# A graph network on one core: part of the row gathers replaced by one-hot matrix products

## The chip, the cores and the metric

The kernel runs on one core of a Trainium2 chip. The core has TensorE (matrix products, PE in the profile; its weight loads are PEld), VectorE (DVE), ScalarE (ACT), GpSimd (POOL) and SyncE (SP), and 16 DMA engines that move data between HBM and on-chip memory: SBUF, and PSUM, which has 8 banks of 512 f32 values in each of 128 partitions. Each engine works through its own instructions in order, and waits on semaphores for the others. The metric is the device time of one execution in microseconds (us), as a median of several.

## The reference

There are 12,500 nodes with 32 features and 400,000 edges `src -> dst`. Three graph attention layers follow one another on the same edges, with a residual and a layernorm; then an edge network with a maximum over the edges of each node, and again a residual and a layernorm.

```python
def _gat(x, edge_index, W, att_s, att_d, bias, heads, ch, neg_slope):
    h = (x @ W.T).reshape(n, heads, ch)
    a_s = (h * att_s[None]).sum(-1)
    a_d = (h * att_d[None]).sum(-1)
    logits = leaky_relu(a_s[src] + a_d[dst], neg_slope)
    m = segment_max(logits, dst)
    ex = exp(logits - m[dst])
    denom = segment_sum(ex, dst)
    alpha = ex / (denom[dst] + 1e-16)
    out = segment_sum(alpha[:, :, None] * h[src], dst)
    return out.reshape(n, heads * ch) + bias
...
x = layernorm(x + three layers of _gat, with elu and clip between them)
e_feat = concatenate([x[rol], x[col], edge_attr])       # rol = src, col = dst
v = relu(e_feat @ W1 + b1) @ W2 + b2
x = layernorm(x + maximum(segment_max(v, col), x))
```

What matters here are the reads by `src`: `h[src]` and `a_s[src]` in each attention layer and `x[rol]` in the edge network, one row of a node table for each of 400,000 edges, four times.

## The kernel before, in words

Edges are sorted by `dst`. Partition p of 128 holds 3125 consecutive edges, so a column t is one edge for each partition. Four stages run over the columns in chunks of T = 60 (50 chunks of 60, then 48, 32, 29 and 16): stages 1 to 3 are `attention(1)`, `(2)` and `(3)` (lines 629 to 784), stage 4 is `edge_network` (lines 805 to 901). For sorted edges the branch without `eid` runs. Sums and maxima over the edges of a node are scans along the columns.

For each column of a chunk, `gather` (line 67, recorded as line 68) issues an indirect DMA from GpSimd's queue: it brings 128 rows of the node table, one for each partition, at the indices `idx[:, t]`. Rows have 36, 34, 33 and 32 f32 values in the four stages. In stages 1 to 3 they land in `g`, of which there are four buffers (line 104); in stage 4 in `xs`, also four (line 832). There is one gather instruction a column, 3125 a stage. In stages 2 to 4 the table is written by the stage before: a table row stands at an edge's place, and `src_last` and `src_first` are the places of a source node's last and first edge; `last_i` and `first_i` hold these places by node. Table rows of chunks and of a last merge go out when they are computed, so a stage's table is complete only at the end of the stage before.

A chunk of attention, in the order of the program: gathers into `g`; the next chunk's `ad` is loaded from SP's queue; `lg` (line 697), scans for the running maximum `mx` (704), `rr` (708 to 711); then `wt`, the exponentials of `lg`, written by ScalarE into `small_p[:, :heads*n]` (715); for each head `rx` (720), the product of `g` with `wt` into `gf` (723) and ScalarE's copy of `wt` into `gf` (725); the scans on `gf` (734); `rows` copied by ScalarE and stored. In stages 1 and 2 `finish` (503) follows: `divided` (487) uses `den = small_p[:, 128:]` and adds the bias (501), which stands in PSUM in the tile `fixed`; three ScalarE passes; then for each block of 16 columns `pe`, `yb`, `yt`, two products on TensorE (`ph` 528, `pa` 529) and transposes by VectorE (531, 532). In stage 3 `finish3` (550) follows: `divided` with the bias from SBUF, the residual, and `layernorm` (537 to 548), whose row sums stand in `small_p` too.

A chunk of stage 4: gathers into `xs`; `keep` in `small_p` (849); `xf` and its scans (854, 864); for each block of 16 columns three transposes (`xt`, `et`, `xst`, 870 to 872), six products into `ph0` and `ph1` (877), two into `pv` (883), and a transpose (884); scans on `vf` (887); then `result` (798), which adds the bias from `fixed`, and `layernorm`, with row sums in `small_p`.

PSUM is full: a tile of up to 512 f32 values takes a bank. `small_p` has a bank of its own, `fixed` another.

At a stage's end `handed_on` (582) carries sums across partitions. Its tile `pt` has two halves in one bank: TensorE transposes `tops` into the second (591), VectorE scans that one (595), and TensorE transposes `nums` into the first (600). Stages 1 and 2 also scatter rows of `x0` into `x_e` there (`move`, 624).

The program is ordered by a list scheduler that gives each engine its instruction order and adds the waits that the order of the program asks for; later instructions fill an engine's gaps where nothing binds them.

Of the kernel before, what the change touches and what calls it, by code (L numbers as in the profile page):

```python
# [9 lines left out]
F32 = mybir.dt.float32  # L10
BF16 = mybir.dt.bfloat16
# [13 lines left out]
def gnn_resnorm_kernel(ctx: ExitStack, tc: tile.TileContext, a: dict, out: bass.AP):  # L25

# [56 lines left out]

    groups = [(c0, min(28, NC - c0)) for c0 in range(0, NC, 28)]
# [19 lines left out]
    gpool = gstack.enter_context(tc.tile_pool(name="g", bufs=4, side="right"))  # L104
# [4 lines left out]
    x0 = runs.tile([P, NC, D], F32, name="x0")  # L109
# [22 lines left out]
    fixed = ctx.enter_context(tc.tile_pool(name="fixed", bufs=1, space=PSUM)).tile([P, 512], F32, name="fixed")  # L132
    own = const.tile([P, 1], F32, name="own")
    nc.gpsimd.iota(own, pattern=[[1, 1]], base=E + NN, channel_multiplier=1,
                   allow_small_or_imprecise_dtypes=True)
    zeros = const.tile([P, 1250], F32, name="zeros")
# [59 lines left out]

    table1 = dram.tile([NN, D + 4], F32, name="table1")
# [10 lines left out]
    def clear(table, part=0, parts=1):  # L208
        flat = edge_rows(table).rearrange("p t w -> p (t w)")
        k = TE * table.shape[1] // parts  # L210
        z = next(z for z in range(1250, 0, -1) if k % z == 0)
        tc.keep_in_program_order(
            nc.sync.dma_start(out=flat[:, part * k:part * k + k].rearrange("p (k z) -> p k z", z=z),
                              in_=bcast(zeros[:, None, :z], [P, k // z, z])))
# [83 lines left out]
    cont = runs2.tile([P, TE + 1], F32, name="cont")  # L298
    src_last = runs2.tile([P, TE], I32, name="src_last")
# [14 lines left out]
    with tc.tile_pool(name="seg", bufs=1) as sp, tc.tile_pool(name="rowsp", bufs=2) as rp, \  # L314
# [52 lines left out]
        for c0, n in groups:  # L367
            rows = rp.tile([P, 28, SB], I32, name="found")
            for c in range(n):
                gather(rows[:, c, :], dst_d, find_i[:, c0 + c:c0 + c + 1])  # L370
            less = rp.tile([P, 28, SB], BF16, name="less")[:, :n, :]
            nc.vector.tensor_tensor(less, rows[:, :n, :], bcast(node_p[:, c0:c0 + n, None], [P, n, SB]), op=ALU.is_lt)
            nc.vector.tensor_reduce(r[:, c0:c0 + n], less, axis=AX.X, op=ALU.add)
            nc.vector.tensor_add(first[:, c0:c0 + n], first[:, c0:c0 + n], r[:, c0:c0 + n])
# [15 lines left out]
        nc.sync.dma_start(out=node_rows(table1), in_=tb)  # L390

# [111 lines left out]
    def finish(li, pool, psum, den, v, n, hb=1):  # L503

        y = pool.tile([P, D * T], F32, name="y")[:, :D * n].rearrange("p (f t) -> p f t", t=n)
        divided(li, y, den, v, n)

        up, down = (scale[:, 0:1], minus[:, 0:1]) if li == 1 else (1.0, -1.0)
        e = pool.tile([P, D * T], F32, name="e", bufs=1)[:, :D * n].rearrange("p (f t) -> p f t", t=n)
        nc.scalar.activation(e, y, AF.Relu, scale=down)  # L510
        nc.scalar.activation(y, y, AF.Relu, scale=up)
        nc.scalar.activation(e, e, AF.Exp, scale=-1.0)
        heads = HEADS[li + 1]
        w_bd, a_bd = weights[li + 1]
        tb = pool.tile([P, T, D + heads], F32, name="tb")[:, :n, :]
        ta = pool.tile([P, T, heads], F32, name="ta")[:, :n, :]
        for b in range(0, n, TB):
            nt = min(TB, n - b)
            w = nt * D
            pe = psum.tile([P, TB * D], F32, name="pe")[:, :w].rearrange("p (f t) -> p f t", t=nt)  # L520
            nc.scalar.activation(pe, e[:, :, b:b + nt], AF.Identity, bias=minus[:, 1:2])  # L521
            yb = pool.tile([P, TB * D], F32, name="yb", bufs=1)[:, :w].rearrange("p (f t) -> p f t", t=nt)
            nc.vector.scalar_tensor_tensor(yb, y[:, :, b:b + nt], 3.0, pe, op0=ALU.min, op1=ALU.add)  # L523
            yt = pool.tile([P, TB * D], F32, name="yt")[:, :w]
            nc.vector.transpose(blocks(yt), yb.rearrange("p f t -> p t f"))  # L525
            ph = psum.tile([P, TB * D], F32, name="ph", bufs=hb)[:, :w]
            pa = psum.tile([P, TB * D], F32, name="pa")[:, :w]
            nc.tensor.matmul(ph, lhsT=w_bd, rhs=yt, start=True, stop=True)  # L528
            nc.tensor.matmul(pa, lhsT=a_bd, rhs=yt, start=True, stop=True)  # L529
            at = pool.tile([P, TB, D], F32, name="at")[:, :nt, :]  # L530
            nc.vector.transpose(tb[:, b:b + nt, :D], blocks(ph))
            nc.vector.transpose(at, blocks(pa))  # L532
            nc.scalar.copy(tb[:, b:b + nt, D:], at[:, :, :heads])  # L533
            nc.scalar.copy(ta[:, b:b + nt, :], at[:, :, heads:2 * heads])
        return tb, ta

    def layernorm(lp, st, x, n):
        st = st[:, :n]
        sq = lp.tile([P, T, D], F32, name="sq", bufs=1)[:, :n, :]
        nc.vector.tensor_reduce(st, x, axis=AX.X, op=ALU.add)  # L540
        nc.vector.tensor_scalar(st, st, 1.0 / D, None, op0=ALU.mult)
        nc.vector.tensor_sub(x, x, bcast(st[:, :, None], [P, n, D]))
        nc.scalar.activation(sq, x, AF.Square)
        nc.vector.tensor_reduce(st, sq, axis=AX.X, op=ALU.add)
        nc.vector.tensor_scalar(st, st, 1.0 / D, EPS, op0=ALU.mult, op1=ALU.add)
        nc.scalar.activation(st, st, AF.Sqrt)
        nc.vector.reciprocal(st, st)
        nc.vector.tensor_mul(x, x, bcast(st[:, :, None], [P, n, D]))  # L548

    def finish3(pool, psum, den, v, x, n):  # L550

        y = psum.tile([P, D * 64], F32, name="y3")[:, :D * n].rearrange("p (f t) -> p f t", t=n)
        divided(3, y, den, v, n)
        nc.vector.tensor_add(x, x, y.rearrange("p f t -> p t f"))
        layernorm(pool, den[:, 2 * T:], x, n)

    def empties():
# [4 lines left out]
        with tc.tile_pool(name="empty", bufs=2) as ep, tc.tile_pool(name="emptyps", bufs=1, space=PSUM) as eps:  # L562
# [66 lines left out]
    def attention(li, idx):  # L629
# [10 lines left out]
        with tc.tile_pool(name=f"s{li}", bufs=2) as sp, tc.tile_pool(name=f"f{li}", bufs=2) as fp:  # L640
# [18 lines left out]
            with tc.tile_pool(name=f"ps{li}", bufs=1, space=PSUM) as psp, \  # L659
                    tc.tile_pool(name=f"fps{li}", bufs=1, space=PSUM) as fps:  # L660

                small_p = psp.tile([P, 512], F32, name="small_p")
                den = small_p[:, 128:]
                old = None
                for c, (t0, n) in enumerate(todo):
                    g = gpool.tile([P, T * (D + 4)], F32, name="g")[:, :n * w].rearrange("p (t w) -> p t w", w=w)
                    for t in range(n):
                        gather(g[:, t, :], table, idx[:, t0 + t:t0 + t + 1])
# [44 lines left out]
                    rx = psp.tile([P, heads, 512], F32, name="rx", bufs=3 - heads)  # L713
# [5 lines left out]
                    for h in range(heads):  # L719
                        nc.scalar.activation(  # L720
                            rx[:, h, :FS * (n + 1)].rearrange("p (k t) -> p k t", t=n + 1),
                            bcast(rr[:, h:h + 1, :], [P, FS, n + 1]), AF.Exp)
                        nc.vector.tensor_mul(v[:, h * wd:h * wd + ch, cur].rearrange("p f t -> p t f"),  # L723
                                             g[:, :, h * ch:(h + 1) * ch], bcast(wt[:, h, :, None], [P, n, ch]))
                        nc.scalar.copy(v[:, h * wd + ch, cur], wt[:, h, :])  # L725
# [4 lines left out]
                    for h in range(heads):  # L730
                        for f in range(0, wd, FS):
                            k = min(FS, wd - f) * (n + 1)
                            o = (h * wd + f) * (n + 1)
                            nc.vector.tensor_tensor_scan(turned(gf[:, o:o + k], rev), turned(rx[:, h, :k], rev),  # L734
                                                         turned(gf[:, o:o + k], rev), 0.0, op0=ALU.mult, op1=ALU.add)
                    rows = sp.tile([P, T, gw + heads], F32, name="rows")[:, :n, :]
# [5 lines left out]
                    if li < 3:  # L742
                        tb, ta = finish(li, fp, fps, den, v[:, :, cur], n, hb=2)
# [61 lines left out]
    def edge_network(tag, in_order):  # L805


        with tc.tile_pool(name=f"in{tag}", bufs=2) as ip, tc.tile_pool(name=f"gx{tag}", bufs=4) as gp, \
                tc.tile_pool(name=f"v{tag}", bufs=2) as vp, tc.tile_pool(name=f"t{tag}", bufs=2) as tp, \
                tc.tile_pool(name=f"pf{tag}", bufs=1, space=PSUM) as pfp, \  # L810
                tc.tile_pool(name=f"ph{tag}", bufs=1, space=PSUM) as php:
            small_p = pfp.tile([P, 512], F32, name="small_p")
# [15 lines left out]

            old = None
            loaded = load(0)  # L830
            for c, (t0, n) in enumerate(todo):
                xs = gp.tile([P, T, D], F32, name="xs")
                for t in range(n):
                    gather(xs[:, t, :], tables[4], src_last[:, t0 + t:t0 + t + 1])
# [31 lines left out]
                for b in range(0, n, TB):  # L866
                    nt = min(TB, n - b)
                    w = nt * D
                    xt, et, st = (tp.tile([P, TB * D], F32, name=x)[:, :w] for x in ("xt", "et", "xst"))
# [29 lines left out]
                layernorm(tp, small_p[:, 128:], z, n)  # L899
# [58 lines left out]
```

## Time and profile before

| | us |
|---|---|
| median of 10 runs | 16351.59 (16349.99 to 16354.64) |
| the profiled execution | 16348.21 |
| its span, first to last instruction | 16346.2 |
| busy: PE, DVE, ACT, POOL | 2752.4, 6832.6, 2898.8, 12192.8 |
| stage 1, first gather to the next stage's first | 303.0 to 4301.0 |
| stage 2 | 4301.0 to 8271.1 |
| stage 3 | 8271.1 to 12222.9 |
| stage 4, to the first gather for the output | 12222.9 to 16216.0 |
| mean granted TensorE clock | 0.578 of full speed |

The span in 40 slices shows how even it is; a digit is the busy share in tenths:

```profile
PE   0111111111111111111100000000003433334342
DVE  2434333333334333333333333333335666665654
POOL 6777777777777777777777777777767777777775
PEclk5555555555555555555555555555556666666676
```

POOL's 75% leaves out the 0.3 us between one gather and the next, which the chain of waits calls issue. The groups list for each line its engine, operation, output and inputs, the count, the busy time and mean ns of one, and the idle time of the engine before it with what ended most of it. Lines in order of time give start, duration, engine, line, operation, out<-in, count, and in brackets the idle time before and its releaser.

### The profile page before, as it was taken

Reading aid. Unit: us, or ns where it says so; the run is one execution under the profiler, and the core shown is the slowest. Engines: PE = TensorE matmul, PEld = TensorE weight load, DVE = VectorE, ACT = ScalarE, POOL = GpSimd, SP = SyncE. Lnnn points to the kernel's source line nnn. Section 1 sums busy time; section 2 is a strip of 40 time slices with the busy share of each in tenths; the row PEclk is TensorE's granted clock in tenths of the full one; section 3 lists DMA queues with packets and bytes.
Section 4 is the critical chain, followed back from the end, with each engine's and each line's share of the span. In section 5 each row is a group of like instructions: output and inputs, shape, how many; then the busy total and the mean of one; then the engine's idle time right before and its main releaser. Section 6 shows DMA issues by size and latency. Waiting matters only on the chain.

```text
span 16346.2 us, 42394 instructions
## 1 busy us (share of the span) xinstructions
PE 2752.4 (17%) x5140; PEld 1114.8 (7%) x5140; DVE 6832.6 (42%) x9700; ACT 2898.8 (18%) x3835; POOL 12192.8 (75%) x12921
## 2 busy tenths in 40 slices
PE   0111111111111111111100000000003433334342
PEld 0000000000000000000000000000001111111110
DVE  2434333333334333333333333333335666665654
ACT  0212222121212121221211111111111111111111
POOL 6777777777777777777777777777767777777775
PEclk5555555555555555555555555555556666666676
DMA  4222222221112121221222222222222222222221
GB/s 60 76 55 73 56 58 71 55 48 43 43 41 47 41 47 41 44 44 42 46 49 56 51 58 51 56 53 56 53 57 59 66 66 64 67 65 64 69 63 42
DMA packets 580809, 897.64 MB, mean 55 GB/s; under 512 B 286270, under 2 KB 490237, under 8 KB 567069
## 3 DMA queue, kind: packets, MB, share of 16 engines
q1 hardware_dynamic: 167116, 665.01, 11.4%
q0 software_dynamic: 413088, 226.62, 11.4%
q10 hardware_dynamic: 304, 3.20, 0.1%
q14 instruction: 259, 2.12, 0.0%
q8 instruction: 42, 0.69, 0.0%
HBM read 390.67 MB, written 503.27 MB: 55 GB/s over the span
## 4 chain that ended last, share of the span: by engine, by line
POOL 71%; issue 23%; DMA 3%; DVE 1%; PE 0%; ACT 0%; POOLq 0%; DVEq 0%; ACTq 0%
POOL g L68 52%; POOL xs L68 17%; DMA g<-table,src_i 1%; DMA g<-table,src_first 1%; DMA g<-table,src_last 1%; DMA xs<-table,src_last 1%; POOL give L72 1%; POOL so L68 1%; POOL x_e L72 1%; PE ph L877 0%; DMA s<-sums,at_i 0%; PE pv L883 0%; DVE vf L887 0%; DVE z L803 0%; ACT xd L889 0%
## 5 line engine op out<-in xcount | busy, mean ns | idle before, releaser
L68 POOL DMA_INDIRECT g<-table,src_i x3125 | 2951.7, 945 | 980.5 <-issue 936.3
L68 POOL DMA_INDIRECT xs<-table,src_last x3125 | 2948.6, 944 | 955.3 <-issue 936.5
L68 POOL DMA_INDIRECT g<-table,src_last x3125 | 2950.8, 944 | 952.4 <-issue 938.0
L68 POOL DMA_INDIRECT g<-table,src_first x3125 | 2949.8, 944 | 952.4 <-issue 938.3
L697 DVE TENSOR_TENSOR lg<-g,af 128x60 f32<-128x60 f32 (+4 forms) x270 | 59.3, 250 | 4411.9 <-DMA g<-table,src_first 2326.7
L528 PE MATMUL ph<-yt,w_bd 128*128 128x512 f32 (+2 forms) x840 | 654.9, 875 | 3429.3 <-DVE yt L525 3429.3
L529 PE MATMUL pa<-yt,a_bd 128*128 128x512 f32 (+2 forms) x840 | 638.4, 854 | 3321.2 <-DVE at L532 3320.5
L683 DVE CAST src_last<-g 128x60 int32<-128x60 f32 (+4 forms) x54 | 12.0, 223 | 2058.6 <-DMA g<-table,src_i 2058.6
L877 PE MATMUL ph<-xt,wb_bd 128*128 128x512 f32 (+2 forms) x832 | 466.6, 646 | 2410.2 <-DVE xt L870 2410.2
L738 ACT COPY rows<-mx 128x120 f32<-128x120 f32 (+3 forms) x162 | 49.9, 308 | 4428.7 <-DVE mx L704 4375.4
L737 ACT COPY rows<-gf 128x2040 f32<-128x2040 f32 (+3 forms) x162 | 628.4, 3879 | 648.5 <-DVE gf L734 648.5
L734 DVE TENSOR_TENSOR_SCAN gf<-rx,gf 128x488 f32<-128x488 f32 (+4 forms) x918 | 731.9, 857 | 1.4 <-ACT gf L725 1.0
L591 PE MATMUL pt<-ident,tops 128*34 128x128 f32 (+1 forms) x3 | 1.0, 323 | 3948.3 <-DVE xr L548 3946.5
L723 DVE TENSOR_TENSOR gf<-g,small_p 128x960 f32<-128x960 f32 (+5 forms) x270 | 597.7, 2214 | 62.8 <-ACT small_p L715 62.7
L523 DVE SCALAR_TENSOR_TENSOR yb<-y,pe 128x512 f32<-128x512 f32 (+2 forms) x420 | 268.8, 640 | 605.4 <-ACT pe L521 586.9
L533 ACT COPY tb<-at 128x32 f32<-128x32 f32 (+4 forms) x420 | 92.3, 220 | 2307.7 <-DVE at L532 2307.7
L879 ACT ACTIVATE ht<-ph,b_c 128x512 f32<-128x512 f32 (+2 forms) x416 | 274.9, 661 | 1149.0 <-PE ph L877 1149.0
L528 PEld LDWEIGHTS ph<-yt,w_bd 128*128 128x128 f32 x840 | 217.3, 287 | 3825.3 <-DVE yt L525 3359.6
L529 PEld LDWEIGHTS pa<-yt,a_bd 128*128 128x128 f32 x840 | 219.2, 277 | 3682.2 <-DVE at L532 3512.6
L877 PE MATMUL ph<-et,wb_bd 128*128 128x512 f32 (+2 forms) x832 | 450.4, 626 | 0.0
L877 PE MATMUL ph<-xst,wb_bd 128*128 128x512 f32 (+2 forms) x832 | 434.2, 605 | 35.9 <-DVE xst L872 35.9
L883 PE MATMUL pv<-ht,w_bd 128*128 128x512 f32 (+2 forms) x832 | 415.4, 593 | 6.0 <-DVE vf L884 1.9
(295 smaller groups left out, 8580.7 us busy)
## 6 DMA issues: line engine op xcount, KB each, us to landing
sums<-rows SPq DMA_DIRECT2D x100, 1080.0 KB, 4.1
table<-tb SPq DMA_DIRECT2D x50, 1020.0 KB, 4.0
sums<-rows SPq DMA_DIRECT2D x50, 1020.0 KB
g<-table,src_i POOLq DMA_INDIRECT x3125
x_e<-zeros SPq DMA_DIRECT2D x10, 5000.0 KB, 15.5
g<-table,src_last POOLq DMA_INDIRECT x3125
g<-table,src_first POOLq DMA_INDIRECT x3125
xs<-table,src_last POOLq DMA_INDIRECT x3125
```

The costliest lines, as they stand in the source:

```text
L68: return nc.gpsimd.indirect_dma_start(out=dst, out_offset=None, in_=table, in_offset=bass.IndirectOffsetOnAxis(ap=idx, axis=0))
L72: return nc.gpsimd.indirect_dma_start(out=table, in_=src, in_offset=None, out_offset=bass.IndirectOffsetOnAxis(ap=idx, axis=0))
L523: nc.vector.scalar_tensor_tensor(yb, y[:, :, b:b + nt], 3.0, pe, op0=ALU.min, op1=ALU.add)
L528: nc.tensor.matmul(ph, lhsT=w_bd, rhs=yt, start=True, stop=True)
L529: nc.tensor.matmul(pa, lhsT=a_bd, rhs=yt, start=True, stop=True)
L533: nc.scalar.copy(tb[:, b:b + nt, D:], at[:, :, :heads])
L723: nc.vector.tensor_mul(v[:, h * wd:h * wd + ch, cur].rearrange("p f t -> p t f"), g[:, :, h * ch:(h + 1) * ch], bcast(wt[:, h, :, None], [ ...
L734: nc.vector.tensor_tensor_scan(turned(gf[:, o:o + k], rev), turned(rx[:, h, :k], rev), turned(gf[:, o:o + k], rev), 0.0, op0=ALU.mult, op1 ...
L737: nc.scalar.copy(rows[:, :, :gw], v[:, :, cur].rearrange("p f t -> p t f"))
L877: nc.tensor.matmul(ph, lhsT=wb_bd[:, s, h, :], rhs=x, start=(s == 1), stop=(s == 0))
L879: nc.scalar.activation(ht, ph, AF.Relu, bias=b1_c[:, h:h + 1])
L883: nc.tensor.matmul(pv, lhsT=w2_bd[:, h, :], rhs=hts[h], start=(h == 0), stop=(h == 1))
```

## The change

Of every 7 columns in stages 1 to 3 and of every 12 in stage 4, the last is no longer gathered. Its rows come from a copy of the node table on the chip, `by_group`: 12,544 node places are cut into 7 groups (KT) of 14 (KN) by column, so a node is at partition q, group k, place b. For such a column, `Fetch.fetch`

- spreads the number `128 k + q` of each edge's node along the free axis by a product with the identity, into `places_p` (128 columns),
- compares that with `kid`, which gives 7 one-hot matrices of 128 x 128 (`oh`, two buffers; the next column's are made before this column's products),
- adds 7 products of a one-hot matrix with a group (14 x width columns of f32) into `acc` (two PSUM buffers, one in stage 4),
- and masks the place b among the 14 by `bm` and sums over them into the column's place in `g` or `xs`.

`rows_of(c + 1)` issues the gathers and the fetch of the next chunk ahead of the work on chunk c. In stage 1 `by_group` is copied from the table that is still in SBUF; ahead of stages 2, 3 and 4 `node_groups` brings it with 98 gathers and 7 copies.

To make room, `small_p` and `places_p` become slices of `fixed`, beside the biases; `g` has 3 buffers for 4; `ph` of `finish` one for two; `rx` is made head by head; `rows`, `y`, `at`, `et` and `xst` have one buffer for two; `zeros` is halved; the layernorm of stage 4 uses `ea` as scratch.

```diff
+    KT, KN = 7, 14
+    EVERY = {1: 7, 2: 7, 3: 7, 4: 12}
...
-    gpool = gstack.enter_context(tc.tile_pool(name="g", bufs=4, side="right"))
+    gpool = gstack.enter_context(tc.tile_pool(name="g", bufs=3, side="right"))
...
+    small_p, places_p = fixed[:, 128:384], fixed[:, 384:]
...
-    zeros = const.tile([P, 1250], F32, name="zeros")
+    kid = const.tile([P, KT], F32, name="kid")
+    nc.gpsimd.iota(kid, pattern=[[P, KT]], base=0, channel_multiplier=1, allow_small_or_imprecise_dtypes=True)
+    zeros = const.tile([P, 625], F32, name="zeros")
...
+    def group(k, rows, w):
+        nc.scalar.copy(by_group[:, k, :KN * w].rearrange("p (w b) -> p w b", b=KN), rows.rearrange("p b w -> p w b"))
+
+    class Fetch:
+        def __init__(self, stack, name, every, w):
...
+            with tc.tile_pool(name=f"{name}t", bufs=1) as fp:
...
+                nc.vector.tensor_copy(node, src_i[:, :m * every].rearrange("p (i c) -> p i c", c=every)[:, :, every - 1])
+                divide(q, r, node, NC, q_i, k)
+                divide(k, self.b, r, KN, q_i, node)
+                nc.vector.scalar_tensor_tensor(self.at, k, float(P), q, op0=ALU.mult, op1=ALU.add)
...
+        def fetch(self, psum, g, t0, n, bufs=2):
+            todo = [t for t in range(t0, t0 + n) if t in self]
...
+            bm = pool.tile([P, 9, KN], F32, name="bm")[:, :len(todo), :]
+            nc.vector.tensor_tensor(bm, bcast(count[:, None, :KN], [P, len(todo), KN]),
+                                    bcast(self.b[:, i0:i0 + len(todo), None], [P, len(todo), KN]), op=ALU.is_equal)
+            def ones_of(m):
+                nc.tensor.matmul(places_p, lhsT=bcast(self.at[:, i0 + m:i0 + m + 1], [P, P]), rhs=ident,
+                                 start=True, stop=True)
+                oh = pool.tile([P, KT, P], F32, name="oh")
+                nc.vector.tensor_tensor(oh, bcast(places_p[:, None, :], [P, KT, P]),
+                                        bcast(kid[:, :, None], [P, KT, P]), op=ALU.is_equal)
+                return oh
+            coming = ones_of(0)
+            for m, t in enumerate(todo):
+                oh = coming
+                if m + 1 < len(todo):
+                    coming = ones_of(m + 1)
+                acc = psum.tile([P, 512], F32, name="acc", bufs=bufs)[:, :KN * w]
+                for k in range(KT):
+                    nc.tensor.matmul(acc, lhsT=oh[:, k, :], rhs=by_group[:, k, :KN * w],
+                                     start=(k == 0), stop=(k == KT - 1))
+                mine = pool.tile([P, D + 4, KN], F32, name="mine")[:, :w, :]
+                nc.vector.tensor_mul(mine, acc.rearrange("p (w b) -> p w b", b=KN),
+                                     bcast(bm[:, m:m + 1, :], [P, w, KN]))
+                nc.vector.tensor_reduce(g[:, t - t0, :w], mine, axis=AX.X, op=ALU.add)
+
+    def node_groups(li, idx, w):
+        with tc.tile_pool(name=f"np{li}", bufs=2) as pool:
+            for k in range(KT):
+                rows = pool.tile([P, KN, D + 2], F32, name="noderows")[:, :, :w]
+                for b in range(KN):
+                    gather(rows[:, b, :], tables[li], idx[:, k * KN + b:k * KN + b + 1])
+                group(k, rows, w)
...
+            fetch = Fetch(stack, f"k{li}", EVERY[li], w)
+            if li > 1 and EVERY[li]:
+                node_groups(li, last_i if li == 2 else first_i, w)
...
-                small_p = psp.tile([P, 512], F32, name="small_p")
                 den = small_p[:, 128:]
-                old = None
-                for c, (t0, n) in enumerate(todo):
+                def rows_of(c):
+                    t0, n = todo[c]
                     g = gpool.tile([P, T * (D + 4)], F32, name="g")[:, :n * w].rearrange("p (t w) -> p t w", w=w)
                     for t in range(n):
-                        gather(g[:, t, :], table, idx[:, t0 + t:t0 + t + 1])
+                        if t0 + t not in fetch:
+                            gather(g[:, t, :], table, idx[:, t0 + t:t0 + t + 1])
+                    fetch.fetch(psp, g, t0, n)
+                    return g
+                old = None
+                coming = rows_of(0)
+                for c, (t0, n) in enumerate(todo):
+                    g = coming
+                    if c + 1 < len(todo):
+                        coming = rows_of(c + 1)
...
-            small_p = pfp.tile([P, 512], F32, name="small_p")
+            fetch = Fetch(stack, f"k{tag}", EVERY[4], D)
+            if EVERY[4]:
+                node_groups(4, last_i, D)
...
+                fetch.fetch(pfp, xs, t0, n, bufs=1)
...
-                    xt, et, st = (tp.tile([P, TB * D], F32, name=x)[:, :w] for x in ("xt", "et", "xst"))
+                    xt, et, st = (tp.tile([P, TB * D], F32, name=x, bufs=k)[:, :w]
+                                  for x, k in (("xt", 2), ("et", 1), ("xst", 1)))
```

## The prediction

> **What bounds the kernel now.** I read the chain of waits first, then the groups, busy time by stage, and single chunks in order of time.
>
> ```profile
> POOL 71%; issue 23%; DMA 3%; DVE 1%; PE 0%; ACT 0%; POOLq 0%; DVEq 0%; ACTq 0%
> ...
> L68 POOL DMA_INDIRECT g<-table,src_i x3125 | 2951.7, 945 | 980.5 <-issue 936.3
> ...
> L68 POOL DMA_INDIRECT xs<-table,src_last x3125: 940/944/961, 12222.9 to 16122.6; - x196
> ```
>
> The chain is GpSimd nearly throughout: a gather is 0.944 us plus 0.30 us of issue. From first to last start in the stage, 3899.7 us / 3124 = 1.248 us a gather (1.258 in stage 1), 75 us a chunk of 60.
>
> ```profile
> core 0: us, PE busy (x) PEld busy (x) DVE busy (x) ACT busy (x) POOL busy (x), PEclk, DMA share, GB/s
> 303.00:4234.00 3931.00, 589.67 (x824) 213.58 (x824) 1473.15 (x2597) 808.60 (x1161) 2950.80 (x3125) 0.56 0.26 59
> 4301.00:8204.00 3903.00, 575.59 (x812) 211.02 (x812) 1412.71 (x2387) 789.30 (x1127) 2950.77 (x3125) 0.57 0.20 43
> 8271.00:12174.00 3903.00, 0.00 (x0) 0.00 (x0) 1383.70 (x1632) 499.95 (x467) 2950.50 (x3126) 0.50 0.23 54
> 12223.00:16122.00 3899.00, 1507.02 (x3280) 650.36 (x3280) 2347.51 (x2566) 718.88 (x871) 2947.26 (x3124) 0.68 0.23 65
> ```
>
> TensorE is idle or nearly so in stages 1 to 3. VectorE has 28 us of work a chunk there, but 45 us in stage 4. So stage 4 has far less room beside its gathers.
>
> ```profile
> 2506.07 0.21 DVE L683 CAST src_last<-g 128x60 int32<-128x60 f32 x1 [38.99 <-DMA g<-table,src_i]
> ...
> 2516.27 0.26 ACT L715 ACTIVATE small_p<-lg 128x120 f32<-128x120 f32 x1
> ...
> 2529.37 2.15 DVE L501 TENSOR_TENSOR y<-y,fixed 128x1920 f32<-128x1920 f32 x1
> ...
> 10074.77 0.22 ACT L715 ACTIVATE small_p<-lg 128x60 f32<-128x60 f32 x1
> ...
> 10100.56 2.15 DVE L548 TENSOR_TENSOR xr<-xr,small_p 128x1920 f32<-128x1920 f32 x1
> ...
> 12521.10 0.22 DVE L849 TENSOR_SCALAR small_p<-cont 128x60 f32<-128x60 f32 x1
> ...
> 12563.76 0.71 DVE L872 STREAM_TRANSPOSE xst<-xs 128x512 f32<-128x512 f32 x1 [5.66 <-DMA xs<-table,src_last]
> ```
>
> These are VectorE and ScalarE in order of time, in one chunk each of stages 1, 3 and 4. In stage 1 VectorE waits 39 us of 75 for gathers. In stage 4 it waits only 5.7 us: the chunk's own chain, from keep (L849) to the layernorm's end (L548), is 74.9 - 5.7 = 69.2 us long.
>
> **What is removed and added.** Removed: 446 gathers in each of stages 1 to 3 (561, 557, 557 us) and 260 in stage 4 (324 us). Added: 98 gathers each ahead of stages 2, 3 and 4, 98 x 1.248 = 122 us, 124 with the last landing and copy. They read a table that is complete only when the stage before has ended, so nothing hides them.
>
> Price of a fetched column. TensorE, from the chain's rows:
>
> ```profile
> 16058.79 5.15 PE ph L877 x12
> ```
>
> Twelve 128x512 f32 instructions take 5.15 us, 0.429 us each at full clock; a product is two instructions. Seven products of 504, 476, 462 or 448 columns cost 14 x 0.429 x width/512 = 5.91, 5.58, 5.42, 5.26 us, and the placing product of 128 columns 0.21. L877's first two instructions after 46 us of idle take 2.08 us, at a granted clock of a half, and full speed comes some 3.6 us later: about 1.8 us lost a burst. VectorE: the comparison is 896 elements at 1.12 ns (L501, 2.15 us / 1920) = 1.0 us, mask and sum of some 500 elements 0.6 us each. A chunk has 8.57 columns (5 in stage 4): 52 us of TensorE and 19 of VectorE in stage 1. By totals all fits under the 64.3 us that 51.4 gathers take.
>
> The Trainium skill (TensorE: Matmul & The Clock Gate, Back-to-back issue gap) gives 216 ns for 512 columns at full clock. The row has twice that per f32 instruction; by the page's figure stages 1 to 3 would stay bound by gathers, as in the second rival.
>
> **The wait that it adds.** places_p, small_p and the biases become slices of one PSUM bank, fixed. Does the placing product, written by TensorE, have to keep off while the others touch other columns? The nearest case is pt:
>
> ```profile
> 12199.63 0.24 ACT L760 COPY nums<-gf 128x33 f32<-128x33 f32 x1
> ...
> 12206.75 0.41 DVE L595 TENSOR_TENSOR_SCAN mxt<-drops,pt 33x128 f32<-33x128 f32 x1 [0.64 <-PE pt L591]
> ...
> 12207.22 0.42 PE L600 MATMUL pt<-ident,nums 128*33 128x128 f32 x1 [0.51 <-DVE mxt L595]
> ```
>
> L600 writes pt's first half from nums, ready 7 us earlier, yet waits until VectorE has read the second half. So an access to a tile of one bank waits for another engine's earlier one, whatever the columns. Its bounds: nothing (the row is a special case: first rival), or full alternation in program order, which I take. The Trainium skill (PSUM — Partial Sum Buffer, PSUM bank collisions raise a hardware error) asks that engines be kept apart by bank, not by address, which speaks against this change; without it one could read the row narrowly and get the first rival's sum.
>
> Program order is: fetch of chunk c+1, then chunk c. So chunk c's first write of small_p (wt, L715; keep, L849 in stage 4) waits for the last placing and comparison of c+1, and the next fetch waits for chunk c's last use (the bias add L501 in stages 1 and 2, L548 in 3 and 4). Behind wt on ScalarE stand both rx and all of finish, on VectorE the product with g; GpSimd then waits for g buffers. The chunk's time is the sum of both phases, unless 64.3 us is longer:
> - Stage 1. Up to the last comparison all but two columns' products are done (two one-hot buffers): 6.57 x 5.91 = 38.8; placings 1.8; first and last comparison 2.2; finish's 16 matmul instructions of the chunk before, in the same queue, 6.4; 3 for clock and handshakes (estimate): 52.2. Then wt to L501: 2531.5 - 2516.3 = 15.3, plus two columns' mask and sum and slack, 2.7: 18. Together 70.2 us.
> - Stage 2, width 476: 36.7 + 1.8 + 2.2 + 6.4 + 3 + 18 = 68.1 us.
> - Stage 3 has no finish products, but cold TensorE and a long second phase: 35.6 + 1.8 + 2.2 + 1.8 + (10102.7 - 10074.8 = 27.9) + 2.7 = 72.0 us.
> - Stage 4: three of five columns 15.8, placings and comparison 2.1, single acc 2 x 0.7, clock and slack 2.1: 21.4; then the chunk's 69.2, plus 2.7 for single et and xst buffers and leftover columns: 93 us, against 75.
>
> **The sum.** 50 full chunks and four short ones count as 52.4 (short instructions shrink less). With node gathers and the ends of stages (40, 40, 30, 15 us; scatters that stood there are free now, GpSimd being ahead), against first gather to first gather before:
> - stage 1: 52.4 x 70.2 + 40 = 3718, before 3998: -280
> - stage 2: 52.4 x 68.1 + 164 = 3732, before 3970: -238
> - stage 3: 52.4 x 72.0 + 154 = 3927, before 3952: -25
> - stage 4: 52.4 x 93 + 139 = 5012, before 3993 (to the first output gather): +1019
>
> Net +476 on the profiled execution's 16348.2 (span 16346.2) is 16824; the median is 3 us above that execution: 16830.
>
> Costed at nothing: the index arithmetic (some 25 VectorE instructions of 446 elements a stage, about 10 us) lies under the 122 us of node gathers; in stage 1 it could cost those 10. Smaller zero rows and single buffers for rows, y and at hide in the tens of us between their uses; three g buffers still leave GpSimd two chunks ahead. The reordered rx costs nothing, since ScalarE's 0.6 us lies under VectorE's scans.
>
> Bounds: without clock and handshake terms 67.2, 65.1, 70.2 and 89 give 16210; 76, 74, 78 and 100 (two-engine queues out of step by half a product every column or so) give 18120.
>
> **Rivals.**
> 1. The bank does not couple them. Gathers then bind stages 1 to 3 (-561, -433, -433 with the added 124), stage 4 is bound by its chain at some 72 us (-27): 14900. For it: all totals fit under 64.3. Against: L600. 13%.
> 2. The other side, with the coupling: phases short enough that gathers stay the bound in stages 1 to 3, stage 4 as forecast: 3437 + 3537 + 3519 + 5012 + 438 = 15940. It decides once the first three stages' mean chunk falls below (11920 - 1019 - 358) / 3 / 52.4 = 67.1 us; I have 70.1. For it: stage 2's lower end is near the floor. Against: stage 3's 28 us second phase. 9%.
> 3. Queues in order: every column shows its whole chain (placing, comparison, products, mask), since VectorE stands before a mask with the next comparison behind it: 2 us more for each of 1338 columns, 19500. For it: VectorE is strictly in order in all timelines. Against: one-hots and acc are doubled in stages 1 to 3. 8%.
>
> **How the numbers follow.** The forecast has 70%; its own range is 16200 to 18120. Leaving out rival 1 and most of 3, the range is 15900 to 18150. 0.2%, 33 us, is about what a measurement can tell from no change. Faster: rivals 1 and 2 and a sliver, 23%; within: 4%; slower: 73%.
>
> **What will show it.** Gathers spread out with GpSimd waiting for g; placing products waiting for L501 or L548, and L715 and L849 for the comparison; stage 4 near 5000 us, the first three near 3700 to 3900; TensorE busy about 12000 us (9250 added) at nearly full clock. GpSimd still back to back at 1.25 us in stages 1 to 3, or stage 4 no longer than before, would make it wrong.

## The result, and the profile after

The changed kernel takes 17173.8 us (median; 17172.1 to 17176.4) against 16352.1 us of the kernel before: a ratio of 1.0503, 95% interval 1.0493 to 1.0512. It is slower by 5.0%, where the forecast had 16830 us (+2.9%).

The chain of waits of the changed kernel, by engine and then by line (L260 are the one-hot products):

```profile
PE 54%; DVE 28%; POOL 8%; issue 4%; ACT 3%; DMA 2%; DVEq 0%; ACTq 0%; POOLq 0%
PE acc L260 40%; PE ph L988 6%; POOL g L70 5%; DVE gf L824 3%; DVE gf L830 3%; PE fixed L246 3%; DVE oh L249 2%; PE pv L994 2%; DVE mine L263 2%; PE ph L611 2%; PE pa L612 2%; POOL noderows L70 1%; DVE y L580 1%; DVE vf L998 1%; DVE fixed L624 1%
```

POOL has gone from 71% of the chain to 8%: the gathers no longer set the time. TensorE and VectorE have taken their place, one after the other, although neither is busy throughout. That shows in the span in 40 slices (busy tenths; PEclk the granted clock):

```profile
PE   0888888886888888885766666764656566565653
...
POOL 6676666666777777767766666665765555555542
PEclk5999999997999999997888888887878888887886
```

The groups say who waits for whom. A line has the busy time, the mean of one instruction in ns, then the idle time ahead of it and what ended most of that:

```profile
L260 PE MATMUL acc<-by_group,oh 128*128 128x504 f32 (+3 forms) x22372 | 9730.3, 587 | 610.7 <-ACT by_group L210 339.2
...
L246 PE MATMUL fixed<-ident,fat 128*128 128x128 f32 x3196 | 785.1, 333 | 3828.5 <-DVE z L632 1633.6
...
L811 ACT ACTIVATE fixed<-lg 128x120 f32<-128x120 f32 (+3 forms) x162 | 41.2, 254 | 5210.7 <-DVE oh L249 5210.4
```

162 short exponentials `wt` (L811, 0.25 us each) stand behind 5210 us of idle ScalarE time, and nearly all of it is ended by the comparison `oh` (L249) of another chunk, whose data they do not use. In return the placing product L246 (the one that spreads the nodes' numbers into `places_p`) waits 1634 us for stage 4's last layernorm instruction, 1082 us for stage 3's and 669 us for the bias add of stages 1 and 2. Both sides touch `fixed`, in different columns.

One chunk of stage 1 in order of time (start, duration, engine, line, operation; in brackets the idle time before and its releaser):

```profile
2097.64 2.14 DVE L584 TENSOR_TENSOR y<-y,fixed 128x1920 f32<-128x1920 f32 x1
...
2099.93 0.77 PE L246 MATMUL fixed<-ident,fat 128*128 128x128 f32 x2 [6.29 <-DVE y L584]
2100.74 1.09 DVE L249 TENSOR_TENSOR oh<-fixed,kid 128x896 f32<-128x896 f32 x1 [0.36 <-PE fixed L246]
...
2155.65 1.08 DVE L249 TENSOR_TENSOR oh<-fixed,kid 128x896 f32<-128x896 f32 x1
...
2156.77 0.27 ACT L811 ACTIVATE fixed<-lg 128x120 f32<-128x120 f32 x1 [32.25 <-DVE oh L249]
```

The fetch phase runs from the end of the bias add (2099.8) to the end of the last comparison (2156.7). Only then `wt` is written, and the use phase ends with the next bias add. The chunk is the sum of the two. From `wt` to `wt` this one takes 73.4 us; others take 66, since a chunk has eight or nine fetched columns.

By stage, from the first gather to the next stage's first (us), with the period of a full chunk, the mean of 42 in a row between successive `wt` or `keep`:

| stage | before | forecast | after | chunk, forecast | chunk, after |
|---|---|---|---|---|---|
| 1 | 3998 | 3718 | 3822 | 70.2 | 70.2 |
| 2 | 3970 | 3732 | 3697 | 68.1 | 67.8 |
| 3 | 3952 | 3927 | 3995 | 72.0 | 73.6 |
| 4 | 3993 | 5012 | 5229 | 93 | 97.3 |

Stages 1 and 2 gain 449 us together, stage 3 loses 43, and the fourth loses 1236.

### The profile page after: what moved, and what is told of

Read it like the earlier page. It is cut to its first block, busy times and chain, and to the rows that moved or that the text cites. A ratio compares the mean times of both kernels' runs of the same rounds, so it can differ in the third digit from the quotient of the medians.

```text
span 17172.6 us, 98222 instructions
## 1 busy us (share of the span) xinstructions
PE 12194.4 (71%) x30708; PEld 5844.1 (34%) x30708; DVE 10400.0 (61%) x14799; ACT 2914.9 (17%) x3863; POOL 10975.4 (64%) x11618
## 4 chain that ended last, share of the span: by engine, by line
PE 54%; DVE 28%; POOL 8%; issue 4%; ACT 3%; DMA 2%; DVEq 0%; ACTq 0%; POOLq 0%
PE acc L260 40%; PE ph L988 6%; POOL g L70 5%; DVE gf L824 3%; DVE gf L830 3%; PE fixed L246 3%; DVE oh L249 2%; PE pv L994 2%; DVE mine L263 2%; PE ph L611 2%; PE pa L612 2%; POOL noderows L70 1%; DVE y L580 1%; DVE vf L998 1%; DVE fixed L624 1%
## 5 line engine op out<-in xcount | busy, mean ns | idle before, releaser
L260 PE MATMUL acc<-by_group,oh 128*128 128x504 f32 (+3 forms) x22372 | 9730.3, 587 | 610.7 <-ACT by_group L210 339.2
L260 PEld LDWEIGHTS acc<-by_group,oh 128*128 128x128 f32 x22372 | 4350.1, 200 | 5046.0 <-issue 4312.9
L263 DVE TENSOR_TENSOR mine<-acc,bm 128x504 f32<-128x504 f32 (+3 forms) x1598 | 1038.1, 650 | 4237.9 <-PE acc L260 4237.3
L246 PE MATMUL fixed<-ident,fat 128*128 128x128 f32 x3196 | 785.1, 333 | 3828.5 <-DVE z L632 1633.6
L70 POOL DMA_INDIRECT g<-table,src_first x2679 | 2529.3, 944 | 1254.6 <-issue 789.6
L70 POOL DMA_INDIRECT g<-table,src_last x2679 | 2531.8, 945 | 961.4 <-issue 793.3
L246 PEld LDWEIGHTS fixed<-ident,fat 128*128 128x128 f32 x3196 | 658.3, 222 | 4536.3 <-issue 2477.1
L249 DVE TENSOR_TENSOR oh<-fixed,kid 128x896 f32<-128x896 f32 x1598 | 1730.5, 1083 | 228.5 <-PE fixed L246 226.9
L811 ACT ACTIVATE fixed<-lg 128x120 f32<-128x120 f32 (+3 forms) x162 | 41.2, 254 | 5210.7 <-DVE oh L249 5210.4
L265 DVE TENSOR_REDUCE g<-mine 128x36 f32<-128x504 f32 (+2 forms) x1338 | 857.5, 641 | 0.2
L824 DVE TENSOR_TENSOR gf<-g,fixed 128x960 f32<-128x960 f32 (+5 forms) x270 | 603.4, 2235 | 1.1 <-ACT fixed L811 1.0
```

The costliest lines, as they stand in the source:

```text
L70: return nc.gpsimd.indirect_dma_start(out=dst, out_offset=None, in_=table, in_offset=bass.IndirectOffsetOnAxis(ap=idx, axis=0))
L246: nc.tensor.matmul(places_p, lhsT=bcast(self.at[:, i0 + m:i0 + m + 1], [P, P]), rhs=ident, start=True, stop=True)
L249: nc.vector.tensor_tensor(oh, bcast(places_p[:, None, :], [P, KT, P]), bcast(kid[:, :, None], [P, KT, P]), op=ALU.is_equal)
L260: nc.tensor.matmul(acc, lhsT=oh[:, k, :], rhs=by_group[:, k, :KN * w], start=(k == 0), stop=(k == KT - 1))
L263: nc.vector.tensor_mul(mine, acc.rearrange("p (w b) -> p w b", b=KN), bcast(bm[:, m:m + 1, :], [P, w, KN]))
L265: nc.vector.tensor_reduce(g[:, t - t0, :w], mine, axis=AX.X, op=ALU.add)
```

## The experiments

Stage times are read in the same way in all of them, from each kernel's profiled execution; the time and the ratio are medians. They are the stretches between the first gathers of the stages, so each of stages 1 to 3 includes the merge at its end.

| kernel | us | ratio to before, 95% interval | stage 1 | 2 | 3 | 4 |
|---|---|---|---|---|---|---|
| own_bank | 15650.3 | 0.957, 0.9554 to 0.9586 | 3585 | 3667 | 3917 | 4074 |
| s4_off | 15932.9 | 0.9743, 0.9727 to 0.9759 | 3827 | 3697 | 3995 | 3984 |
| every8 | 15243.7 | 0.9322, 0.9306 to 0.9337 | 3533 | 3609 | 3697 | 3973 |
| every10 | 15427.9 | 0.9418, 0.9403 to 0.9434 | 3615 | 3704 | 3677 | 3973 |
| empties2 | 17174.9 | 1.0503, 1.0486 to 1.0521 | 3822 | 3697 | 3995 | 5229 |
| empties_later | 17231.8 | 1.0519, 1.0501 to 1.0536 | 3740 | 3832 | 3995 | 5232 |
| one_product | 15500.0 | 0.9462, 0.9446 to 0.9477 | 3458 | 3543 | 3528 | 4538 |
| own_psum7 | 15265.8 | 0.9321, 0.9305 to 0.9336 | 3752 | 3578 | 3500 | 3976 |
| psum877 | 14996.5 | 0.9175, 0.916 to 0.919 | 3517 | 3576 | 3499 | 3972 |
| psum_rx | 14902.4 | 0.9117, 0.9102 to 0.9132 | 3450 | 3542 | 3500 | 3975 |

### The small tiles and biases leave the bank

Theory: the shared bank makes the two phases alternate. Rival: it does not, and the time is TensorE's and VectorE's own work. own_bank keeps every fetch and moves what the rest of the chunk touches into SBUF.

```diff
-    small_p, places_p = fixed[:, 128:384], fixed[:, 384:]
+    places_p = fixed[:, 384:]
+    sums_s = const.tile([P, P], F32, name="sums_s")
-        biases[li] = fixed[:, D * (li - 1):D * li]
+        biases[li] = b_all[:, li - 1, :]
-                den = small_p[:, 128:]
+                den = sums_s
-                    wt = small_p[:, :heads * n].rearrange("p (h t) -> p h t", t=n)
+                    wt = before[:, :heads * n].rearrange("p (h t) -> p h t", t=n)
-                keep = small_p[:, :n]
+                keep = before[:, :n]
-                layernorm(tp, small_p[:, 128:], z, n, ea)
+                layernorm(tp, sums_s, z, n, ea)
```

> The changed kernel with the sums, wt, keep and the biases in SBUF, so that only the placing product and its comparison touch the bank. Bank theory: ScalarE's wait for the comparison goes; stages 1 to 3 are bound by gathers at about 64.4 us a chunk of 60 (3560 us each with node gathers or the late start), stage 4 by its own chain at about 75 us a chunk (4060 us); together 15200 us. Rival, TensorE's 12.2 ms of work is what binds: within 2% of 17174 us, since TensorE does the same work. Rival, VectorE's strict order (mask ahead of the next work) binds: 16800 us or more.

It took 15650.3 us: the slowdown is gone, and the kernel is 4.3% faster than the one before with the same fetches. The coupling is the cause of the loss. Stage 4 falls from 5229 to 4074 us, which is still 81 more than before the change: its fetches gain nothing even then. The 450 us that are missing to the expectation were not explained by any theory then. They lie in the gathers. First GpSimd's group for the 2679 gathers of stage 3 in own_bank, then gathers and VectorE instructions of one chunk of it in order of time:

```profile
L70 POOL DMA_INDIRECT g<-table,src_first x2679 | 2943.1, 1099 | 816.8 <-issue 802.7 <-DMA g<-table,src_first 14.0
```

```profile
9049.76 3.77 DVE L825 TENSOR_TENSOR gf<-g,before 128x1920 f32<-128x1920 f32 x1 [1.30 <-ACT before L812]
9050.41 3.79 POOL L70 DMA_INDIRECT g<-table,src_first  x1 [0.30 <-issue]
...
9062.97 2.17 DVE L581 TENSOR_TENSOR y<-gf,sums_s 128x1920 f32<-128x1920 f32 x1
9063.25 2.69 POOL L70 DMA_INDIRECT g<-table,src_first  x1 [0.30 <-issue]
...
9065.17 2.17 DVE L585 TENSOR_TENSOR y<-y,b_all 128x1920 f32<-128x1920 f32 x1
...
9076.00 2.16 DVE L627 TENSOR_TENSOR xr<-xr,sums_s 128x1920 f32<-128x1920 f32 x1
9076.26 2.72 POOL L70 DMA_INDIRECT g<-table,src_first  x1 [0.30 <-issue]
...
9085.08 2.16 DVE L633 TENSOR_TENSOR xr<-xr,sums_s 128x1920 f32<-128x1920 f32 x1
9085.53 2.53 POOL L70 DMA_INDIRECT g<-table,src_first  x1 [0.30 <-issue]
```

Four gathers of a chunk last 2.5 to 3.8 us instead of 0.944, and each begins during a VectorE product whose two inputs both stand in SBUF, and ends 0.7 to 0.8 us after it. L585, as long, holds up none in this stage: its `y` stands in PSUM. The extra is 3.79 + 2.69 + 2.72 + 2.53 - 4 x 0.944 = 7.95 us a chunk, 417 us in 52.4 chunks; stage 3 of own_bank is 417 us longer than that of own_psum7 below. In all of own_bank 662 gathers last over 1.5 us, nearly all of them beside VectorE products of this kind; in the changed kernel it is one. The Trainium skill (SBUF — State Buffer, Who interferes with whom) has a VectorE instruction with two SBUF inputs contend with a GpSimd instruction that reads SBUF; these rows agree, with an indirect DMA as the GpSimd side.

### The places get a bank of their own

own_psum7 uncouples the two the other way round, to test that reading: `small_p` and the biases stay in PSUM, `places_p` gets a bank, for which `acc` gives up one of its two. Stage 4 has no bank to spare and fetches nothing.

```diff
-    EVERY = {1: 7, 2: 7, 3: 7, 4: 12}
+    EVERY = {1: 7, 2: 7, 3: 7, 4: 0}
-    small_p, places_p = fixed[:, 128:384], fixed[:, 384:]
+    small_p = fixed[:, 128:384]
+            places_p = psum.tile([P, 512], F32, name="placed", bufs=1)[:, :P]
             def ones_of(m):
-                    fetch.fetch(psp, g, t0, n)
+                    fetch.fetch(psp, g, t0, n, bufs=1)
```

> Only the placed indices get a PSUM bank of their own (stages 1 to 3; the bank is paid for by a single acc buffer), the small tiles and biases stay in PSUM, stage 4 fetches nothing. If the own_bank version lost its missing 450 us because VectorE read the moved tiles from SBUF and held up GpSimd's gathers, the gathers go back to 1.248 us each, stages 1 to 3 take about 3560, 3520 and 3510 and the whole is about 15030 us. If the gathers were slowed by anything else that the uncoupled kernel does, they stay at 1.30 to 1.40 us and the whole is own_bank with the stage 4 of before, about 15570 us.

It took 15265.8 us, between the two times expected. The gathers are back at 944 to 948 ns in all stages, and stages 2 and 3 take 3578 and 3500 us, so the reading of own_bank holds. Stage 1 alone is long: 3752 us, 68.6 us a chunk. TensorE in a chunk of stage 1 of own_psum7, in order of time:

```profile
2086.35 0.38 PE L248 MATMUL placed<-ident,fat 128*128 128x128 f32 x2
2089.46 6.18 PE L262 MATMUL acc<-by_group,oh 128*128 128x504 f32 x14 [2.73 <-DVE mine L265]
2095.48 0.38 PE L248 MATMUL placed<-ident,fat 128*128 128x128 f32 x2
2098.74 7.82 PE L262 MATMUL acc<-by_group,oh 128*128 128x504 f32 x14 [2.87 <-DVE mine L265]
```

With one `acc` the products wait for VectorE's mask (`mine`), which stands behind the chunk's scans, and TensorE, busy 3254 us of the stage's 3753, has little to spare. Two kernels test that: psum877 fetches one column in 8 in stage 1 alone; psum_rx keeps two `acc` buffers and gives up one of two `rx` in stages 1 and 2. Both were first run as own_psum877 and own_psum_rx, on a chip where the kernel before itself took 18531 us instead of 16352; they took 22970 and 22472 us there, and nothing is read from that pair.

psum877, against own_psum7:

```diff
-    EVERY = {1: 7, 2: 7, 3: 7, 4: 0}
+    EVERY = {1: 8, 2: 7, 3: 7, 4: 0}
```

> The kernel of own_psum877 again: there the kernel before itself took 18531 us instead of 16352, so nothing could be read from the pair. One column in 8 in stage 1, one in 7 in stages 2 and 3, places in a PSUM bank of their own with one acc buffer. If TensorE bounds own_psum7 only in stage 1 (68.8 us a chunk), that falls to the gathers' 65.5 us and the whole to about 15045 us; if stage 1 is held by something else, it stays near 15240.

psum_rx, against own_psum7:

```diff
-                    fetch.fetch(psp, g, t0, n, bufs=1)
+                    fetch.fetch(psp, g, t0, n, bufs=2 if li < 3 else 1)
...
-                        rx = psp.tile([P, 512], F32, name="rx", bufs=heads)
+                        rx = psp.tile([P, 512], F32, name="rx", bufs=1)
```

> The kernel of own_psum_rx again, for the same reason: two acc buffers and one rx buffer in stages 1 and 2. If the single acc buffer stretched stage 1 of own_psum7, a chunk falls from 68.8 us to 65 or 66 and the whole to about 15090 us; if the products alone fill the chunk, or the single rx buffer costs as much, it stays at 15240 to 15270.

psum877 took 14996.5 us (stage 1 3517 us, with the gathers back to back) and psum_rx 14902.4 (stage 1 3450): the single `acc` was it, and the second `rx` is free. psum_rx beats both kernels, the one before by 8.8%; part of that is that it fetches nothing in stage 4 (s4_off, below). Its chain of waits, and its busy time by stage (us, then PE, PEld, DVE, ACT and POOL busy with instruction counts, granted clock, DMA share, GB/s):

```profile
POOL 65%; issue 22%; DVE 5%; DMA 4%; PE 3%; ACT 1%; POOLq 0%; DVEq 0%; ACTq 0%
```

```profile
303.00:3754.00 3451.00, 3174.67 (x7994) 1442.09 (x7994) 2532.15 (x4126) 837.74 (x1209) 2592.25 (x2733) 0.97 0.27 66
3754.00:7295.00 3541.00, 3103.08 (x7976) 1455.86 (x7976) 2427.94 (x3895) 818.23 (x1182) 2678.87 (x2830) 0.95 0.19 47
7295.00:10795.00 3500.00, 2792.94 (x7134) 1381.80 (x7134) 2353.35 (x3098) 525.14 (x502) 2625.43 (x2782) 0.92 0.22 59
10795.00:14770.00 3975.00, 1532.24 (x3330) 661.16 (x3330) 2397.12 (x2688) 735.92 (x903) 2950.47 (x3128) 0.68 0.21 64
```

The gathers set the time again. TensorE is busy 3175 of 3451 us in stage 1, 92%, so one column in 7 is about what it can take (an estimate from that share).

### Stage 4 without fetches, fewer fetches

The bank stays shared in these three; s4_off, every8 and every10 have, in this order, for `EVERY = {1: 7, 2: 7, 3: 7, 4: 12}`:

```diff
+    EVERY = {1: 7, 2: 7, 3: 7, 4: 0}
...
+    EVERY = {1: 8, 2: 8, 3: 8, 4: 0}
...
+    EVERY = {1: 10, 2: 10, 3: 10, 4: 0}
```

> The changed kernel with no fetched columns and no node gathers in stage 4 alone. Bank theory: stage 4 returns to the 3993 us of before, stages 1 to 3 stay at 3822, 3697 and 3994 us; 15940 us in all, faster than before. Rival, stage 4 lost by the smaller buffers (single et, xst, shared scratch): stage 4 stays over 4300 us, 16250 us or more.

15932.9 us, as expected: stage 4 alone gave away 1241 us, and stages 1 to 3 did not move. s4_off also is the pair to psum_rx: the same columns are fetched, and only the bank and one `rx` and one `acc` buffer differ, 15932.9 against 14902.4. The alternation costs 377, 155 and 495 us in stages 1, 2 and 3 (the fewer `rx` and `acc` buffers of psum_rx could only have made it slower).

> As the kernel with stage 4 off, but one column in 8 fetched, not one in 7, in stages 1 to 3. Bank theory: the two phases add to 64 us a chunk in stage 1, 62 in stage 2 and 66 in stage 3, so that the 52.5 gathers of a chunk (65.6 us) bind: 3630, 3590 and 3620 us, 15260 us in all, faster than with more columns fetched. Rival, time goes with the number of gathers that are left (56 more in each of three stages, 1.25 us each): 16150 us, slower than the kernel with stage 4 off.

15243.7 us. Fewer fetched columns are faster, although more rows are gathered: a shorter fetch phase shortens the sum. With 1.07 columns less a chunk, stage 3 fell by 298 us.

> One column in 10 in stages 1 to 3, none in stage 4. If one in 8 is already bound by the gathers, 1.5 more gathers a chunk cost 1.9 us on some 53 chunks in three stages: 15244 + 300 = 15540 us. If one in 8 still waited for the shared bank, fewer fetched columns would shorten it further, and this would be 15244 us or less.

15427.9 us, 184 slower than every8 instead of 300 (159 between the two profiled executions). Stages 1 and 2 paid 82 and 95 us for 78 more gathers each (78 x 1.248 = 97), so they were bound by gathers at one in 8; stage 3 fell by 20. At one in 8 its chunks still took 67.7 us, over the 65.5 of 52.5 gathers: in stage 3 the phases still bound. The "already bound" theory was right for two stages of three.

### The price of the products, with the coupling kept

```diff
-                for k in range(KT):
+                for k in range(1):
...
-                                     start=(k == 0), stop=(k == KT - 1))
+                                     start=True, stop=True)
```

> Six of the seven one-hot products of each fetched column are left out (so the output lacks the node rows of six groups of seven); the shared bank and every comparison stay. If a chunk is the sum of a fetch phase and a use phase, and TensorE's products are most of the first, stages 1 to 3 fall under the gathers' 64.4 us a chunk and stage 4 to about 80 us: about 15330 us. If the wait were the alternation itself, whatever the products cost, stages would stay near 70, 67 and 74 us a chunk and the whole above 16700 us.

15500.0 us. Stages 1 to 3 (3458, 3543, 3528) fall to within 28 us of what psum_rx has (3450, 3542, 3500), with the alternation still in place: it costs next to nothing where the sum of the phases stays under the gathers. Stage 4 was expected at 80 us a chunk and has 83.7:

```profile
13924.38 2.15 DVE L632 TENSOR_TENSOR z<-z,fixed 128x1920 f32<-128x1920 f32 x1
13927.42 1.09 DVE L249 TENSOR_TENSOR oh<-fixed,kid 128x896 f32<-128x896 f32 x1 [0.89 <-PE fixed L246]
13929.40 1.09 DVE L249 TENSOR_TENSOR oh<-fixed,kid 128x896 f32<-128x896 f32 x1 [0.89 <-PE fixed L246]
...
13936.29 1.08 DVE L249 TENSOR_TENSOR oh<-fixed,kid 128x896 f32<-128x896 f32 x1
13938.34 0.21 DVE L959 TENSOR_SCALAR fixed<-cont 128x60 f32<-128x60 f32 x1
```

From the layernorm's end (13926.5) to `keep` (13938.3) the fetch phase is 12 us long with one product of seven left in each column. In the changed kernel it takes 24.5 us, so leaving out six products of seven shortens it by no more than half; the rest is the one product, the placings, the comparisons and the waits between the two engines.

### The late start of stage 1

In the changed kernel VectorE starts the index arithmetic of the first fetch only at 430.5 us, 128 us after the first gather. The line is from it, the two after it from empties2, both in order of time:

```profile
430.54 0.56 DVE L227 CAST fn<-src_i 128x446 f32<-128x446 int32 x1 [2.37 <-DMA table<-z]
```

```profile
399.38 1.09 DVE L654 TENSOR_TENSOR z<-x,fixed 128x896 f32<-128x896 f32 x1 [63.86 <-DMA table<-z]
432.21 0.61 DVE L227 CAST fn<-src_i 128x446 f32<-128x446 int32 x1 [2.09 <-DMA table<-z]
```

It stands behind `empties`, the rows of nodes without edges, which waits for its own stores twice (28.9 and 33.5 us). empties2 gives it two buffers; empties_later calls it after stage 1.

```diff
-        with tc.tile_pool(name="empty", bufs=1) as ep, tc.tile_pool(name="emptyps", bufs=1, space=PSUM) as eps:
+        with tc.tile_pool(name="empty", bufs=2) as ep, tc.tile_pool(name="emptyps", bufs=1, space=PSUM) as eps:
...
-    empties()
     attention(1, src_i)
+    empties()
```

> The changed kernel with two buffers in place of one for the rows of empty nodes at the start of stage 1. If VectorE's waits for these rows' stores (28.9 and 34.0 us in its order of time) hold up the first fetch: stage 1 about 100 us shorter, 17070 us. Rival, the first fetch waits for something else (the index arithmetic, by_group): no change, 17174 us.

Nothing moved (17174.9 us): the two waits became one of 63.9 us. L227 still waits for the last store of `z`, which is none of its data. By the order of the pools its tiles probably stand in memory that `empties` gave back; no run shows that.

> The rows of the nodes without edges are made after stage 1 instead of before it. If the first fetch of stage 1 was held up until 430 us by them, it runs within the first chunk's gathers, the first weights come near 400 us instead of 542, and stage 2 hides the work behind its 98 node rows and first gathers: about 17060 us. If the late start came from elsewhere, or stage 2 does not hide them, 17150 to 17180 us.

Half right. The first `wt` came at 420 us instead of 542, but stage 1 fell by 82 us only: the first gather of stage 2, with which it ends, waited 42 us for a store of empty rows into its table. And stage 2 grew by 135: the node rows came only at 4208 us, 164 us after that gather, and ScalarE stood 105 us for them before its first copy into `by_group`. The whole is 58 us slower.

## Why the prediction was right, and where its sizes were off

**The bank couples the two.** Right, and shown twice: own_bank keeps all fetches and takes the sharing away, and the loss of 5.0% turns into a gain of 4.3%; psum_rx fetches the same columns as s4_off without the sharing, and is 1030 us faster. That a wait on L600 for the other half of `pt` would carry over to `fixed` was read from one row of the old trace, a wait of 0.51 us. The rule of the Trainium skill that it was weighed against (PSUM — Partial Sum Buffer, PSUM bank collisions raise a hardware error) points the same way: the 5210 us of waits at L811 are between engines that touch different columns of one bank. The tile `fixed` fills one bank, as `pt` has one, so no run here tells whether the waits go by the tile or by the bank.

**The chunk is the sum of both phases.** Right; the terms for stages 1 and 2 (70.2 and 68.1 us) met 70.2 and 67.8. That they met so closely is partly luck: in stage 1 the fetch phase took 53.8 us for 52.2 and the use phase 16.4 for 18, in stage 2 51.4 for 50.1 and 16.4 for 18. Three terms were mis-sized, and with stage 2's -35 they make up the 344 us between forecast and result but for some 10:
- Stage 4, +217: 97.3 us a chunk for 93. The fetch phase is 24.5 us, not 21.4: the first two placings and comparisons follow each other with TensorE waiting for the first comparison (1.18 us) ahead of any product, and after 32 us of waiting the first column's products take 7.04 us at a mean granted clock of 0.77, the next ones 5.53. The rest is 72.7, not 71.9, in turn 71.9 and 73.6: the last column's products wait 3.79 us for a mask that stands behind the scans of `xf`, and in every other chunk they then take 7.22 us at a granted clock of 0.76 instead of 5.53 at 1.00. The blocks' products stand behind them, 15 us after `keep` in such a chunk.
- Stage 1, +104: chunks as forecast, but 40 us for the stage's ends were too little; they took some 143. What stood ahead of the first fetch was not looked for: VectorE's work on the empty rows. The prediction had allowed the index arithmetic 10 us here. empties_later took 82 us of it out of stage 1.
- Stage 3, +68: 73.6 us a chunk for 72.0. The use phase was as forecast (30.2 against 27.9 + 2.7), the fetch phase 2 us longer, with the same start of two placings one after the other.

Stage 4 of the changed kernel in order of time, with the two waits of 1.18 and 3.79 us that the forecast left out:

```profile
14031.22 0.80 PE L246 MATMUL fixed<-ident,fat 128*128 128x128 f32 x2 [31.75 <-DVE z L632]
...
14033.20 0.80 PE L246 MATMUL fixed<-ident,fat 128*128 128x128 f32 x2 [1.18 <-DVE oh L249]
14033.79 7.04 PE L260 MATMUL acc<-by_group,oh 128*128 128x448 f32 x14
...
14055.42 0.21 DVE L959 TENSOR_SCALAR fixed<-cont 128x60 f32<-128x60 f32 x1
...
14063.36 7.22 PE L260 MATMUL acc<-by_group,oh 128*128 128x448 f32 x14 [3.79 <-DVE mine L263]
```

**The prices.** TensorE is busy 12194 us (forecast about 12000). One column's placing and products in stage 1 take 6.14 us from start to start, forecast 5.91 + 0.21. The row gave two f32 instructions of 0.43 us a product, and so it is.

**The rivals.** The first, no coupling, was wrong for this kernel, but its sum was right for a kernel without it: it had 3437, 3537 and 3519 us for stages 1 to 3, and psum_rx has 3450, 3542 and 3500. The second needed a mean chunk under 67.1 us in these stages; it is 70.5. The third, 2 us more a column, did not come: from the second column on, placing and comparison lie under the products.

## What to carry to other kernels

When tiles are packed into one PSUM bank to make room, ask which engines touch the bank and in what program order: with an engine that works a chunk ahead, a packed bank makes the two chunks alternate, and the price is the sum of both phases wherever that exceeds the bound. Count a bank for the tile that works ahead, and find it where a second buffer earns nothing (here the second `rx`). And price moved work by the stage: in stage 4 the same edit that pays in stages 1 and 2 lengthened a chain that had 6 us to spare.

## What had not been expected of the hardware

- An indirect DMA's issue on GpSimd is held up by VectorE products with both inputs in SBUF: 0.944 us becomes 2.5 to 3.8, and own_bank's stage 3 lost 417 us by it. With the small tiles in PSUM, as before, the same products leave the gathers at 0.944 us.
- The mean granted TensorE clock is higher where TensorE is busier: 0.578 in the kernel before (busy 17% of the span), 0.66 in one_product, where most products are left out (33%), 0.852 in the changed kernel (71%), and 0.97 in stage 1 of psum_rx (92%).
